# Phase two's full-array products issued as four tiles of 32 columns

## The chip, the cores and the metric

The kernel runs on one core of a Trainium2 chip. The metric is the device time of one execution in microseconds; lower is better. Times before are the median of three runs. The profile is one execution, recorded by the hardware profiler.

## What is computed

The input `x` has 8 sequences of 1024 tokens with 256 features. All is f32. Two blocks follow each other, each with a residual:

```python
x = x + attn_ref(layernorm(x))     # phase one: 16 heads, low-rank keys and values, causal
x = x + ffn_ref(layernorm(x))      # phase two: two layers, DEPTH = 2

def layer(x):                      # 8 heads of 64, windows of 128 tokens
    h = shift_token(x)             # second half of the features is taken from the token before
    q, k, v = split(h @ wqkv, 3)   # 256 -> 3 * 512
    q, k = rotary_xpos(l2norm(q) * qs, l2norm(k) * ks)
    o = local_attention(q, k, v)   # a window sees itself and the window before
    x = x + o @ wo                 # 512 -> 256
    h = layernorm(shift_token(x)) * g + b
    a, gate = split(h @ w1 + b1, 2)        # 256 -> 2 * 682
    return x + (a * gelu(gate)) @ w2 + b2  # 682 -> 256
```

Phase two's two layers over eight sequences are 16 passes. Each has 8 windows of 128 tokens for the attention (128 windows in all) and 2 chunks of 512 tokens for the MLP (32 chunks in all).

## The kernel before

Phase one (`mla`) takes about the first 967 us. Its dense products already go through a helper `times` (L199), which issues a product of 128 x 128 weights as four matmuls, one for each 32 columns of the weights, into the four 32-partition strips of the output. Its scores (L455) use 32 rows and 128 columns of the array, its values (L488) 128 rows and 32 columns.

Phase two (`local`) is the part that changes. A class `Pass` holds one layer of one sequence. Its methods work on a window `i`:

- `qk` (product at L886): q and k of the window, four products of 128 x 128 weights (the tokens, transposed, `left(i)`) with 512 moving columns of `wqkv`, into a PSUM pair buffer `pair`. ScalarE squares it (L891), VectorE multiplies by the rotary tables (L893, L896), GpSimd adds and scales (L900, L906).
- `transposes`: a turn on VectorE and a way through DRAM by SyncE's DMA queue (`turned`, `z`, `qkT`).
- `v` (L913): two such products, evacuated by ScalarE.
- `scores` (L958): 32 matmuls in tiles of 64 rows and 32 columns into two more turns of the pair buffers, which ScalarE reads with the exponential (L964).
- `values` (L999) and the sums of the softmax (L1007): 32 and 8 matmuls in tiles of 128 rows and 32 columns.
- `output` (L1032), once for two windows: 16 is the number of its recorded matmuls, 128 x 128 weights with 256 moving columns.

The MLP of a chunk is a generator, `mlp`, advanced in units between these: `up` (L1115), 128 x 128 weights with 512 moving columns, then Gelu (L1127) on ScalarE and the gated product (L1128) on VectorE; and the down projection `psy`, L1156 with 128 x 128 weights and 256 moving columns, and at its end the rest of the hidden features, L1162, which has 64 rows (one half of `rest_hid` for each of two sums).

The order on every compute engine is that of the program text (`tc.manual_schedule`). A step of the main loop works on several windows at once, each at another stage:

```python
each(step, "both", 4); each(step, "qk", 0); each(step, "transposes", 1); each(step, "v", 0)
next(units, None)             # a unit of the MLP
each(step, "values", 4)
each(step, "scores", 3)
made[j // NT].output(...)     # every second step
next(units, None)             # a unit of the MLP
```

So in each step TensorE goes from full-array products to `values`, its sums and `scores`, and back to full-array products. Two pair buffers (`pair0`, `pair1`) take turns for `qk` once and `scores` twice in a step; three banks (`mm`) serve v, the sums, output and the MLP. An f32 product appears in the profile as two matmuls and two weight loads.

Of the kernel before, what the change touches and what calls it, by code (L numbers as in the profile page):

```python
# [36 lines left out]
P = 128  # L37
# [21 lines left out]
INNER = HEADS * DH  # L59
# [23 lines left out]
def preln_mla_local_kernel(  # L83
# [27 lines left out]
    nc = tc.nc  # L111
# [12 lines left out]
    def rsqrt(out_, in_, n):  # L124

        nc.gpsimd.tensor_tensor(out_, in_, half[:, :n], ALU.pow)  # L126
# [527 lines left out]
    NF = HID // P  # L654
# [3 lines left out]
    def local(ctx: ExitStack, verdict):  # L658
# [4 lines left out]
        p1 = ctx.enter_context(tc.tile_pool(name="l1", bufs=1))  # L663
        p2 = ctx.enter_context(tc.tile_pool(name="l2", bufs=2))

        ppair = [ctx.enter_context(tc.tile_pool(name="pair0", bufs=1, space=PSUM))]
        psum = ctx.enter_context(tc.tile_pool(name="psum3", bufs=3, space=PSUM))
        ppair.append(ctx.enter_context(tc.tile_pool(name="pair1", bufs=1, space=PSUM)))
# [7 lines left out]
        rest_hid = p1.tile([P, CH // 2], F32, name="rest_hid")  # L676
# [12 lines left out]
        def load_attention(l):  # L689


            w = {}
            queue = nc.sync if l else nc.scalar
            w["qkv"] = wa.tile([P, 2, 3 * INNER], F32, tag="qkv", name=f"l_qkv{l}")
            nc.sync.dma_start(w["qkv"], wqkv[l].rearrange("(c p) e -> p c e", p=P))

            for name, src in (("cos", xpos_cos), ("sin", xpos_sin)):
                w[name] = wa.tile([P, NT, 2, DH], F32, tag=name, name=f"l_{name}{l}")
                queue.dma_start(w[name], src)
                f = wa.tile([P, 2, DH], F32, tag=f"f{name}", name=f"l_f{name}{l}")  # L700
                for i, sc_ in enumerate((q_scale, k_scale)):
                    if name == "cos":
                        queue.dma_start(f[:, i, :], sc_[l].partition_broadcast(P))
                    else:
                        queue.dma_start(f[:, i, :H], sc_[l, H:].partition_broadcast(P))
                        queue.dma_start(f[:, i, H:], sc_[l, :H].partition_broadcast(P))
                w[f"f{name}"] = f
            return w
# [156 lines left out]
        class Pass:  # L865
# [14 lines left out]
            def qk(self, i):  # L880
                key, w = self.key(i), self.w
                A, S = w["cos"], w["sin"]
                qk = next(turns).rearrange("p (n j) (m d) -> p n (j m) d", n=2, d=DH)
                for n in range(2):
                    for c in range(2):
                        nc.tensor.matmul(  # L886
                            qk[:, n].rearrange("p h d -> p (h d)"), self.left(i)[c],
                            w["qkv"][:, c, n * INNER : (n + 1) * INNER], start=(c == 0), stop=(c == 1),
                        )
                sq = p1.tile([P, 2, HEADS, DH], F32, tag="sq", name=f"sq{key}")  # L890
                nc.scalar.activation(sq, qk, AF.Square)  # L891
                t1 = p1.tile([P, 2, HEADS, DH], F32, tag="t1", name=f"t1{key}", bufs=2)
                nc.vector.tensor_tensor(t1, qk, A[:, i].unsqueeze(2).to_broadcast([P, 2, HEADS, DH]), ALU.mult)  # L893
                t2 = p1.tile([P, 2, HEADS, DH], F32, tag="t2", name=f"t2{key}")
                for lo, hi in ((0, H), (H, 0)):
                    nc.vector.tensor_tensor(  # L896
                        t2[:, :, :, lo : lo + H], qk[:, :, :, hi : hi + H],
                        S[:, i, :, lo : lo + H].unsqueeze(2).to_broadcast([P, 2, HEADS, H]), ALU.mult,
                    )
                nc.gpsimd.tensor_tensor(t1, t1, t2, ALU.add)  # L900
                ss = small.tile([P, 2, HEADS], F32, tag="ss", name=f"ss{key}")
                nc.vector.tensor_reduce(ss, sq, AX.X, ALU.add)
                nc.vector.tensor_scalar(ss, ss, 1e-24, None, ALU.max)
                rn = small.tile([P, 2, HEADS], F32, tag="rn", name=f"rn{key}")
                rsqrt(rn.rearrange("p i h -> p (i h)"), ss.rearrange("p i h -> p (i h)"), 2 * HEADS)
                nc.gpsimd.tensor_tensor(t1, t1, rn.unsqueeze(3).to_broadcast([P, 2, HEADS, DH]), ALU.mult)  # L906
                self.rot[i] = t1

            def v(self, i):
                key = self.key(i)  # L910
                pv = psum.tile([P, INNER], F32, tag="mm", name=f"pv{key}")
                for c in range(2):
                    nc.tensor.matmul(  # L913
                        pv, self.left(i)[c], self.w["qkv"][:, c, 2 * INNER :], start=(c == 0), stop=(c == 1)
                    )
                self.vs[i] = p1.tile([P, INNER], F32, tag="v", name=f"v{key}", bufs=6)
                evac(self.vs[i], pv)

# [105 lines left out]
            def output(self, n):  # L1024

                oT = self.oTs.pop(n)
                x_, y, key = self.x_, self.y, f"{self.b}_{self.l}"
                two = slice(2 * n, 2 * n + 2)
                ps = psum.tile([P, 2, D], F32, tag="mm", name=f"psw{key}_{n}")
                for i in range(2):  # L1030
                    for c in range(4):
                        nc.tensor.matmul(  # L1032
                            ps[:, i, :], oT[:, c, i * P : (i + 1) * P], self.w["o"][:, c, :],
                            start=(c == 0), stop=(c == 3),
                        )
                nc.vector.tensor_tensor(x_[:, two], ps, x_[:, two], ALU.add)  # L1036

                rows = slice(2 * n * P, (2 * n + 2) * P)
                nc.sync.dma_start(y[rows, :P].rearrange("(t p) d -> p t d", p=P), x_[:, two, :P])
                rows = slice(2 * n * P + 1, (2 * n + 2) * P + 1)  # L1040
                nc.sync.dma_start(y[rows, P:].rearrange("(t p) d -> p t d", p=P), x_[:, two, P:])
                m, o = divmod(2 * n + 2, ST)
                if o == 0:
                    self.hs[m - 1] = p2.tile([P, ST, D], F32, tag="h", name=f"h{key}_{m - 1}")
                    rows = slice((m - 1) * CH, m * CH)
                    nc.sync.dma_start(self.hs[m - 1], y[rows].rearrange("(t p) d -> p t d", p=P))
# [49 lines left out]
        def mlp():  # L1096


            w = load_mlp(0)
# [7 lines left out]
            for k, (q, n) in enumerate(chunks):  # L1107
                l, b, x_ = made[q].l, made[q].b, made[q].x_
                key = made[q].key(n)
                d = ds.pop(k)  # L1110

                def up(i):
                    ps = psum.tile([P, CH], F32, tag="mm", name=f"ag{key}_{i}")
                    for c in range(2):
                        nc.tensor.matmul(  # L1115
                            ps.rearrange("p (s a t) -> p s a t", a=4, t=32), w["1"][:, c, i, :],
                            d[:, c],
                            start=(c == 0), stop=(c == 1),
                        )
                    return ps  # L1120

                hid = p1.tile([P, NF, CH], F32, tag="hid", name=f"hid{key}")
                for i in range(NF):
                    gate = up(2 * i + 1)
                    a = up(2 * i)
# [14 lines left out]
                for g in range(2):  # L1140
                    cols = slice(CH // 2 * g, CH // 2 * (g + 1))
# [10 lines left out]
                for g, ps in enumerate(sums):  # L1152
                    for t in range(2):
                        cols = slice((2 * g + t) * P, (2 * g + t + 1) * P)
                        for i in range(NF):
                            nc.tensor.matmul(  # L1156
                                ps[:, t, :], hid[:, i, cols], w["2"][:, i, :], start=(t == i == 0), stop=False
                            )
                for t in range(2):
                    for g, ps in enumerate(sums):  # L1160
                        rows = slice(64 * g, 64 * g + 64)
                        nc.tensor.matmul(  # L1162
                            ps[:, t, :], rest_hid[rows, t * P : (t + 1) * P], w["2"][rows, NF, :], start=False,
                            stop=(t == 1),
                        )
                for g, ps in enumerate(sums):
                    part = slice(ST * n + 2 * g, ST * n + 2 * g + 2)
# [3 lines left out]
                    else:  # L1171
                        rows = slice(n * CH + 2 * g * P, n * CH + (2 * g + 2) * P)
# [4 lines left out]
                if k + 1 < len(chunks) and made[chunks[k + 1][0]].l > l:  # L1177
                    w = load_mlp(l + 1)
# [17 lines left out]
        w = load_attention(0)  # L1196
# [3 lines left out]
        ready = {0: first}  # L1200
        w["o"] = load_o(0)
        units = mlp()
        next(units)

# [7 lines left out]
        with tc.manual_schedule(engines={E.PE, E.DVE, E.Activation, E.Pool}):  # L1212
            for step in range(windows + LAG):
                n, i = divmod(step, NT)
                if step < windows and i == 0:
                    l, b = passes[n]
                    if n and b == 0:
                        o = w["o"]
                        w = load_attention(l)
# [556 lines left out]
    with ExitStack() as two:  # L1776
        local(two, verdict)
# [7 lines left out]
    with tc.tile_pool(name="psum_v", bufs=1, space=PSUM) as psum:  # L1785
        ps = psum.tile([1, 1], F32, name="psbad")
# [80 lines left out]
```

## Time and profile before

| | |
|---|---|
| median of three runs | 3293.98 us (3292.47 to 3296.29) |
| the profiled execution: time | 3292.07 us |
| its span, first to last instruction | 3290.3 us |
| mean granted TensorE clock | 0.994 |
| instructions | 79693 |
| recorded matmuls, and weight loads | 33762 each |
| phase two (967 us to the end) | 23458 matmuls, as many loads |

The full-array products of phase two, each group with its matmuls, its busy time and the mean length of one:

| line | product | matmuls | moving columns | busy us | mean ns |
|---|---|---|---|---|---|
| L1115 | MLP up | 1408 | 512 | 640.8 | 597 |
| L886 | q, k | 1024 | 512 | 466.7 | 599 |
| L1156 | MLP down | 1280 | 256 | 281.5 | 379 |
| L913 | v | 512 | 512 | 240.6 | 592 |
| L1032 | attention output | 1024 | 256 | 240.2 | 388 |
| L1162 | MLP down, rest (64 rows) | 256 | 256 | 36.3 | 402 |

PE is TensorE's matmuls, PEld its weight loads, which overlap with them. DVE is VectorE, ACT ScalarE, POOL GpSimd, SP SyncE. A matmul's length is longer than its share of the engine, since the next starts before it ends; so the distance from one start to the next is what tells its cost. In shapes like `128*32 128x512`, the first pair is the rows and columns of the array that are used, the second the moving operand.

### The profile page before, as it was taken

The page shows a single profiled execution, that of the slowest core. Times are in us where ns is not written, and L with a number is a line of the kernel's source. Part 1 is how long each engine was busy: PE and PEld are TensorE (multiplying, and loading weights), DVE is VectorE, ACT ScalarE, POOL GpSimd, SP SyncE. Part 2 cuts the span into 40 slices and gives each one's busy share as a digit, 9 for nine tenths or more (in the row PEclk, how much of TensorE's full clock was granted, in tenths as well). Part 3 has the DMA queues.
Part 4 walks back from the last instruction along what each step waited for, and adds up shares of the span by engine and source line. Part 5 has one row for each costly group of instructions (what it writes and reads, how often), then busy time and mean ns, then how long its engine had stood idle before and what let it go on. Part 6 is the DMA issues. An engine that isn't in the chain of part 4 may idle for free.

```text
span 3290.3 us, 79693 instructions
## 1 busy us (share of the span) xinstructions
PE 3196.2 (97%) x33762; PEld 1763.2 (54%) x33762; DVE 2668.6 (81%) x3934; ACT 1712.4 (52%) x2055; POOL 1342.9 (41%) x1064
## 2 busy tenths in 40 slices
PE   7999999999987999999999999999999999999998
PEld 2434343443334566656666656566666656665665
DVE  4999989998987887887878877787877778787773
ACT  6888888888742344444343444343443444444441
POOL 1000000000017755555555555565555555555540
PEclk9999999999998999999999999999999999999999
DMA  4133222313324344444445445454544535454431
GB/s 128 44 94 84 59 75 75 91 46 84 105 89 114 101 128 119 132 118 119 121 117 135 112 128 145 126 129 137 148 123 122 142 110 134 133 139 123 112 102 58
DMA packets 389771, 362.10 MB, mean 110 GB/s; under 512 B 158703, under 2 KB 337310, under 8 KB 389278
## 3 DMA queue, kind: packets, MB, share of 16 engines
q1 hardware_dynamic: 387422, 354.51, 39.8%
q8 instruction: 268, 4.39, 0.6%
q10 hardware_dynamic: 1984, 2.41, 0.2%
q14 instruction: 97, 0.79, 0.1%
HBM read 165.96 MB, written 140.51 MB: 93 GB/s over the span
## 4 chain that ended last, share of the span: by engine, by line
PE 84%; DVE 6%; ACT 4%; DMA 2%; issue 2%; SPq 1%; POOL 0%; ACTq 0%; DVEq 0%
PE ag L1115 17%; PE pair L886 13%; PE psy L1156 8%; PE psw L1032 7%; PE o L999 6%; PE acc L488 6%; PE pv L913 6%; PE sc L455 5%; PE pair L958 4%; DVE pt L477 3%; PE s L1007 2%; PE psx L201 2%; PE psq L201 1%; PE psR L201 1%; ACT pt L463 1%
## 5 line engine op out<-in xcount | busy, mean ns | idle before, releaser
L477 DVE TENSOR_TENSOR pt<-pt,er 128x1024 f32<-128x1024 f32 x576 | 671.7, 1221 | 35.8 <-ACT pt L463 35.7
L1115 PE MATMUL ag<-d,l 128*128 128x512 f32 x1408 | 640.8, 597 | 1.4 <-DVE xs L1036 0.8
L900 POOL TENSOR_TENSOR t<-t,t 128x1024 f32<-128x1024 f32 x128 | 302.0, 2360 | 791.5 <-DVE t L896 791.5
L463 ACT ACTIVATE pt<-sc 128x1024 f32<-128x1024 f32 x576 | 561.2, 1032 | 115.6 <-PE sc L455 105.9
L964 ACT ACT_TABLE_LOAD x120 | 154.0, 1283 | 701.2 <-PE pair L958 697.1
L886 PE MATMUL pair<-l_qkv,xT 128*128 128x512 f32 x1024 | 466.7, 599 | 5.7 <-DMA xT<-zx 2.8
L1115 PEld LDWEIGHTS ag<-d,l 128*128 128x128 f32 x1408 | 262.0, 190 | 311.0 <-issue 276.9
L126 POOL TENSOR_TENSOR rn<-ss,half 128x16 f32<-128x16 f32 x128 | 373.4, 2917 | 13.8
L488 PE MATMUL acc<-pt,v 128*32 128x512 f32 (+3 forms) x3072 | 345.6, 496 | 11.2 <-DVE pt L477 10.0
L886 PEld LDWEIGHTS pair<-l_qkv,xT 128*128 128x128 f32 x1024 | 193.1, 191 | 247.5 <-issue 208.8
L891 ACT ACTIVATE sq<-pair 128x1024 f32<-128x1024 f32 x128 | 131.1, 1024 | 330.7 <-issue 256.5
L893 DVE TENSOR_TENSOR t<-pair,l_cos 128x1024 f32<-128x1024 f32 x128 | 156.3, 1221 | 155.6 <-ACT sq L891 155.0
L1156 PE MATMUL psy<-l,hid 128*128 128x256 f32 x1280 | 281.5, 379 | 0.0
L1128 DVE SCALAR_TENSOR_TENSOR hid<-ag,l_b,ge 128x512 f32<-128x512 f32 x160 | 115.9, 724 | 195.4 <-ACT ge L1127 170.4
L1156 PEld LDWEIGHTS psy<-l,hid 128*128 128x128 f32 x1280 | 243.2, 190 | 46.7 <-issue 15.1
L964 ACT ACTIVATE pt<-pair 128x1024 f32<-128x1024 f32 (+1 forms) x256 | 235.0, 968 | 57.1 <-PE pair L958 55.8
L906 POOL TENSOR_TENSOR t<-t,rn 128x1024 f32<-128x1024 f32 x128 | 249.1, 1946 | 10.0
L455 PE MATMUL sc<-q,k 32*128 32x512 f32 (+3 forms) x3072 | 245.1, 380 | 4.4 <-ACT pt L463 3.3
L999 PEld LDWEIGHTS o<-pt,v 128*32 128x32 f32 x7680 | 201.6, 110 | 88.0 <-issue 82.0
L913 PE MATMUL pv<-l_qkv,xT 128*128 128x512 f32 x512 | 240.6, 592 | 0.0
L1032 PE MATMUL psw<-l_o,oT 128*128 128x256 f32 x1024 | 240.2, 388 | 0.0
L999 PE MATMUL o<-pt,v 128*32 128x128 f32 x7680 | 237.0, 274 | 2.6 <-POOL pt L966 2.4
(324 smaller groups left out, 4604.0 us busy)
## 6 DMA issues: line engine op xcount, KB each, us to landing
z<-turned SPq DMA_DIRECT2D x512, 128.0 KB, 2.4
qkT<-z SPq DMA_DIRECT2D x128, 512.0 KB, 3.6
y<-xs SPq DMA_DIRECT2D x128, 128.0 KB, 3.4
h<-y SPq DMA_DIRECT2D x32, 512.0 KB, 4.3
zx<-turneds SPq DMA_DIRECT2D x120, 128.0 KB, 2.4
xT<-zx SPq DMA_DIRECT2D x240, 64.0 KB, 2.6
zh<-turnedh SPq DMA_DIRECT2D x120, 128.0 KB, 2.3
d<-zh SPq DMA_DIRECT2D x30, 512.0 KB, 3.2
```

The source lines that it names most:

```text
L126: nc.gpsimd.tensor_tensor(out_, in_, half[:, :n], ALU.pow)
L455: nc.tensor.matmul(two[n // 2][:, n % 2, lo : lo + w], k[rows], q[rows, h], start=(h == 1), stop=(h == 0),)
L463: nc.scalar.activation(pt, sc, AF.Exp, scale=SCALE)
L477: nc.vector.tensor_tensor(t, t, er.to_broadcast([P, 1024 // w, w]), ALU.mult)
L488: nc.tensor.matmul(self.acc[g][32 * n : 32 * n + 32, q0 - c * 512 :], self.v[:, kb, h * VW : h * VW + 32], pts[n // 2][:, n % 2, lo : lo + w],
L886: nc.tensor.matmul(qk[:, n].rearrange("p h d -> p (h d)"), self.left(i)[c], w["qkv"][:, c, n * INNER : (n + 1) * INNER], start=(c == 0), s ...
L913: nc.tensor.matmul(pv, self.left(i)[c], self.w["qkv"][:, c, 2 * INNER :], start=(c == 0), stop=(c == 1))
L964: nc.scalar.activation(pt[:, :, : n * P], flat[:, :, : n * P], AF.Exp, scale=-1.0)
L999: nc.tensor.matmul(o[32 * j : 32 * j + 32, g, a, :], vs[m][:, h * DH + a * 32 : h * DH + a * 32 + 32], pts[m][g][:, place(j), off : off + ...
L1032: nc.tensor.matmul(ps[:, i, :], oT[:, c, i * P : (i + 1) * P], self.w["o"][:, c, :], start=(c == 0), stop=(c == 3),)
L1115: nc.tensor.matmul(ps.rearrange("p (s a t) -> p s a t", a=4, t=32), w["1"][:, c, i, :], d[:, c], start=(c == 0), stop=(c == 1),)
L1156: nc.tensor.matmul(ps[:, t, :], hid[:, i, cols], w["2"][:, i, :], start=(t == i == 0), stop=False)
```

## The change

`local` gets its own `times`, the same as that of phase one, and every product that used all 128 columns is issued through it. The weights' 128 columns are taken 32 at a time, and the output's partitions likewise; the moving operand, the accumulation and the order of the products stay. The tiles have 128 rows and 32 columns, and for L1162 64 rows and 32 columns.

```diff
+        QUARTER = [slice(32 * n, 32 * n + 32) for n in range(4)]
+
+        def times(out, w, rhs, start, stop):
+            for four in QUARTER:
+                nc.tensor.matmul(out[four], w[:, four], rhs, start=start, stop=stop)
+
...
                 for n in range(2):
                     for c in range(2):
-                        nc.tensor.matmul(
+                        times(
                             qk[:, n].rearrange("p h d -> p (h d)"), self.left(i)[c],
-                            w["qkv"][:, c, n * INNER : (n + 1) * INNER], start=(c == 0), stop=(c == 1),
+                            w["qkv"][:, c, n * INNER : (n + 1) * INNER], c == 0, c == 1,
                         )
...
                 for c in range(2):
-                    nc.tensor.matmul(
-                        pv, self.left(i)[c], self.w["qkv"][:, c, 2 * INNER :], start=(c == 0), stop=(c == 1)
-                    )
+                    times(pv, self.left(i)[c], self.w["qkv"][:, c, 2 * INNER :], c == 0, c == 1)
...
                 for i in range(2):
                     for c in range(4):
-                        nc.tensor.matmul(
-                            ps[:, i, :], oT[:, c, i * P : (i + 1) * P], self.w["o"][:, c, :],
-                            start=(c == 0), stop=(c == 3),
-                        )
+                        times(ps[:, i, :], oT[:, c, i * P : (i + 1) * P], self.w["o"][:, c, :], c == 0, c == 3)
...
                     for c in range(2):
-                        nc.tensor.matmul(
-                            ps.rearrange("p (s a t) -> p s a t", a=4, t=32), w["1"][:, c, i, :],
-                            d[:, c],
-                            start=(c == 0), stop=(c == 1),
+                        times(
+                            ps.rearrange("p (s a t) -> p s a t", a=4, t=32), w["1"][:, c, i, :], d[:, c],
+                            c == 0, c == 1,
                         )
...
                         for i in range(NF):
-                            nc.tensor.matmul(
-                                ps[:, t, :], hid[:, i, cols], w["2"][:, i, :], start=(t == i == 0), stop=False
-                            )
+                            times(ps[:, t, :], hid[:, i, cols], w["2"][:, i, :], t == i == 0, False)
                 for t in range(2):
                     for g, ps in enumerate(sums):
                         rows = slice(64 * g, 64 * g + 64)
-                        nc.tensor.matmul(
-                            ps[:, t, :], rest_hid[rows, t * P : (t + 1) * P], w["2"][rows, NF, :], start=False,
-                            stop=(t == 1),
+                        times(
+                            ps[:, t, :], rest_hid[rows, t * P : (t + 1) * P], w["2"][rows, NF, :], False, t == 1
                         )
```

## The prediction

> **What bounds the kernel now.** I read four views: the page's busy table, the stretches, the chain of waits, and the timeline of TensorE. Phase one ends and phase two begins at about 967 us; the second line below is the table of stretches cut there, its columns being span, then busy time and instructions of PE, PEld, DVE, ACT, POOL.
>
> ```profile
> PE 3196.2 (97%) x33762; PEld 1763.2 (54%) x33762; DVE 2668.6 (81%) x3934; ACT 1712.4 (52%) x2055; POOL 1342.9 (41%) x1064
> ...
> PE 84%; DVE 6%; ACT 4%; DMA 2%; issue 2%; SPq 1%; POOL 0%; ACTq 0%; DVEq 0%
> ```
> ```profile
> 967.00:3290.00 2323.00, 2283.49 (x23458) 1396.28 (x23458) 1814.14 (x2864) 932.91 (x1013) 1263.61 (x932) 0.99 0.44 122
> 1100.00:3200.00 2100.00, 2095.53 (x21726) 1282.43 (x21725) 1671.81 (x2636) 880.12 (x949) 1160.00 (x858) 1.00 0.46 126
> ```
>
> From 1100 to 3200 us PE is busy for 2095.5 of 2100 us, and the next engine, DVE, for 1672 (80%). The chain is 84% PE. So PE sets the time of phase two, at full clock (1.00), and a nanosecond taken off PE is one off the span, unless a wait turns up in its place. But busy is not the same as full speed. The timeline (start us, length us, what) shows where PE is slower than its own steady pace. One window's stretch in phase two:
>
> ```profile
> 2015.29 1.13 PE L1162 MATMUL psy<-l,rest_hid 64*128 64x256 f32 x8
> 2016.35 1.95 PE L999 MATMUL o<-pt,v 128*32 128x128 f32 x64
> 2018.12 0.62 PE L1007 MATMUL s<-both,ones_l 128*32 128x128 f32 x16
> 2018.67 1.32 PE L958 MATMUL pair<-qkT 64*32 64x160 f32 x64
> 2019.92 3.72 PE L1032 MATMUL psw<-l_o,oT 128*128 128x256 f32 x16
> 2023.48 3.60 PE L886 MATMUL pair<-l_qkv,xT 128*128 128x512 f32 x8
> 2026.91 1.88 PE L913 MATMUL pv<-l_qkv,xT 128*128 128x512 f32 x4
> 2028.63 3.60 PE L1115 MATMUL ag<-d,l 128*128 128x512 f32 x8
> 2032.15 1.96 PE L999 MATMUL o<-pt,v 128*32 128x128 f32 x64
> ```
>
> Read start to start, since lengths overlap. An f32 product is two recorded matmuls. L886 takes 3.43 us for 8: 429 ns each, its steady pace at 512 columns; at 256 the trace's starts are 216 apart. L1115 takes 3.52 us for the same 8, 93 more: after it L999 uses another shape of the array (128*128 to 128*32). L1032 takes 3.56 us where 16 x 216 is 3.46: its first matmul holds PE 104 ns longer, having been entered from another shape, so its weight load was not hidden. L999 after such an entry takes 1.77 us for 16 rounds of four at 109, which is 24 more: its loads have 32 columns. L1162 has both ends, 1.06 us for four rounds of 215.
>
> And phase one, where products are already issued as four tiles:
>
> ```profile
> 604.14 1.05 PE L201 MATMUL psx<-wout,oT 128*32 128x256 f32 x16
> 605.00 1.04 PE L436 MATMUL reach<-sq,ones_m 128*32 128x512 f32 x8
> 605.97 0.75 PE L455 MATMUL sc<-q,k 32*128 32x256 f32 x16
> ```
>
> 16 tiles of 256 columns take 0.86 us, with no change of shape after them: 215 ns for each four. 8 tiles of 512 take 0.97 with a change after them: 2 x 429 + 0.11 (93 for the change, 20 for the stagger of the last four). Taken one by one, starts in phase one are 7 ns apart within a four, and fours are 429 or 216 apart: the pace of the full array.
>
> **What the skill says.** The Trainium skill, "TensorEngine Tiling (Array Packing)", Key Properties: "Changing tiling mode (not just tile) drains the TensorE". The trace agrees and prices it: 93 ns on every such change. "TensorE: Matmul & The Clock Gate", LDWEIGHTS: a load costs its column count over 1.2, so 107 ns at 128 columns and 27 at 32; the exposed loads above are 104 and 24. The same page, Part 3 (packing), has tiles in different column strips running together, about 4 ns apart; the trace has them together, 7 apart.
>
> **The change part by part.** A "round" is one pass through PE: one full matmul now, four tiles afterwards.
>
> 1. *Steady pace.* Full matmuls by the groups: 1408 + 1024 + 1280 + 1024 + 512 = 5248 become 20992, and L1162's 256 become 1024: 16512 more matmuls and as many loads. Rounds stay 5248, at 429 or 216 ns either way: cost 0. What hides four times the instructions is their concurrency. Phase one doesn't show the moving pattern of L1115 (runs of 32 elements), but L958 reads such runs in eight tiles together at 136 ns a round for 160 columns, no slower in proportion. Bounds: a round 1 ns shorter or 2 ns longer, -5 to +10 us; I take 0.
>
> 2. *Into L999.* Each of 128 windows has L999, L1007, L958. Into L999 PE comes 98 times from a full product, which will then have the same shape: drain 93 and exposed load 24 go, 98 x 117 = 11.5 us. In 30 windows it comes from L1162, which keeps a shape of its own (64*32 hereafter), so nothing goes.
>
> 3. *Out of L958.* 64*32 to full becomes 64*32 to 128*32: the drain stays, the exposed load falls from 104 to 24. The trace counts 130 such entries: 130 x 80 = 10.4 us. No row has 64*32 to 128*32; nearest are 64*128 to 128*32 (93 + 24) and 128*32 to 64*32 (93 + 24), so I take 93 + 24.
>
> 4. *L1162.* Still entered over a drain, but with 32-column loads: 32 x 80 = 2.6 us. Its 64-row halves must still run together in eight tiles as L958's do; if one half trailed by a round, it would cost 32 x 215 ns = 6.9 us. Bounds -2.6 to +4.3; I take the gain.
>
> 5. *Waits after L958.* In 28 windows the q, k product waits for the pair buffer that the exponential still reads:
>
> ```profile
> PE pair L958 <- DMA qkT<-z: 15.1, 4, 9.4
> ```
> ```profile
> PEld pair L886 <- ACT pt L964: 31.7, 55, 1.2
> ```
>
> (Waited for: us in total, times, longest.) The first is the largest of PE's waits in phase two, for item 6; the second, from 1100 to 3200 us, is that of L886's weight loads; behind it the whole PE queue stands, v and the next unit of the MLP. The 80 ns of item 3 come after L958, so here PE only arrives earlier and waits longer: -28 x 80 ns = 2.2 us lost. But each restart exposes its load too (104 more in 28 rounds of L886), now 24: 2.2 us won back. Net 0. Item 2 comes before L958 and moves the exponential as well, so it isn't absorbed.
>
> 6. *Start of phase two.* The four waits for qkT, 15.1 us, are mostly a chain of DMAs before the first windows. Some five windows' worth of 0.2 us vanishes there: +1 us.
>
> DMAs, their order on SP, and the work of DVE, ACT and POOL are unchanged. The only added traffic is instructions: see the slower rival.
>
> Sum: -11.5 - 10.4 - 2.6 + 0 + 1 = -23.5 us. The profiled execution took 3292.07 us (span 3290.3 and 1.8 around it), so 3268.6; it lies 1.9 below the median of the runs, 3293.98, and from that I get **3270.5 us** (-0.7%). About 0.2%, 6.6 us, is what a measurement of this kernel can tell from no change.
>
> **Rivals.**
>
> *A: waits take it back.* PE's cover is thin after L958: ACT's table load (1283 ns) and two exponentials (971 each) follow it, and only some windows have slack. If all of item 3 and half of item 2 ended in waits, 23.5 falls to 7.4: 3286.6. For it: the 55 waits on that buffer. Against it: they sum to only 31.7 us, most windows have an output or more of the MLP between, and DVE is idle a fifth of the time.
>
> *B: slower; instructions arrive too late.* Phase two has 23458 matmuls and as many loads in 2323 us, 20 instructions a us; with 16512 more of each it is 34. The instruction queue (q8) moved 4.39 MB in 268 packets for 67524 PE instructions, so 16 KB and some 250 instructions a packet, at 0.6% of 16 engines: 1.2 us each. Needed hereafter is one in 7 us. That speaks against it, as does the burst of 144 matmuls and 144 loads in 3.6 us (L999 to L958) at 80 a us. For it: no stretch of 100 us has over 25 a us now. It decides below 34 a us; at 33.5, phase two's 79940 would take 2386 us, 63 longer than now: 3357. A milder form is a round that is longer by tile overhead: the saving is gone at 23.5 us over 5248 rounds, 4.5 ns each; at 7 ns it is +37 - 23.5, or 3307.
>
> *C: the tiles don't run together.* Each four would take four rounds, thousands of us in all. The same helper in phase one (0.86 us for 16 tiles) excludes it.
>
> **How the numbers follow.** Forecast 0.75, A 0.15, B 0.1, C 0. The forecast's own range is 3262 (a round 1 ns shorter and some waits shorter) to 3281 (rounds 2 ns longer). A extends it to 3287; B is left out. Range 3262 to 3287. Faster by over 0.2% means below 3287.4: the forecast and most of A, 0.86. Within 0.2%: 0.05. Slower: 0.09.
>
> **What would show it.** PE has 50274 matmuls. Before L999, eight matmuls of L1115 become 32 in 3.43 us instead of 3.52; L1032 after L958 takes 3.48 instead of 3.56; L1162 has 32 in 0.98 instead of 1.06 (1.2 or more if its halves trail). L886's loads waiting for ACT stay near 32 us; at 45 or more, A is at work. Rounds of 436 or 223, or PE idle for issue, would mean B. The forecast is wrong if fours in phase two are over 4 ns longer than full matmuls, or if L958 to a 128*32 tile costs more than 93 + 24.

## The result, and the profile after

The changed kernel takes 3275.4 us, median of six runs (3272.52 to 3276.37), against 3293.22 for the kernel before in six: ratio 0.9942, 95% interval 0.9932 to 0.9953, a gain of 17.8 us. The forecast was 3270.5 (23.5 us of gain) with a range of 3262 to 3287. The profiled execution has a span of 3273.5 us, 16.8 less than before.

The busy table and the chain of waits of the changed kernel:

```profile
PE 3177.2 (97%) x50274; PEld 1456.0 (44%) x50274; DVE 2671.1 (82%) x3934; ACT 1712.5 (52%) x2055; POOL 1341.6 (41%) x1064
...
PE 84%; DVE 6%; ACT 4%; DMA 3%; issue 2%; SPq 1%; POOL 0%; ACTq 0%; DVEq 0%; POOLq 0%
```

The 16512 added matmuls are there (33762 to 50274), with their loads. PE lost 19 us of busy time and its weight loads (PEld) 307; VectorE, ScalarE and GpSimd changed by under 3. The chain is still 84% PE: no other engine took over. Phase two as one stretch (start and end, span, then busy time of PE, PEld, DVE, ACT, POOL, with their instructions, the granted clock, and the DMA share and rate):

```profile
967.00:3273.00 2306.00, 2264.21 (x39970) 1088.57 (x39970) 1816.21 (x2863) 933.21 (x1013) 1262.30 (x932) 0.99 0.45 124
```

PE handles 39970 matmuls and as many loads in 2306 us, 35 instructions a us. The timeline of PE (start us, length us, what) in the place that answers to the one shown of before:

```profile
2005.63 1.09 PE L670 MATMUL psy<-l,rest_hid 64*32 64x256 f32 x32
2006.65 1.95 PE L1003 MATMUL o<-pt,v 128*32 128x128 f32 x64
2008.42 0.62 PE L1011 MATMUL s<-both,ones_l 128*32 128x128 f32 x16
2008.97 1.45 PE L962 MATMUL pair<-qkT 64*32 64x160 f32 x64
2010.35 3.66 PE L670 MATMUL psw<-l_o,oT 128*32 128x256 f32 x64
2013.83 3.62 PE L670 MATMUL pair<-l_qkv,xT 128*32 128x512 f32 x32
2017.26 1.90 PE L670 MATMUL pv<-l_qkv,xT 128*32 128x512 f32 x16
2018.98 3.62 PE L670 MATMUL ag<-d,l 128*32 128x512 f32 x32
2022.41 1.93 PE L1003 MATMUL o<-pt,v 128*32 128x128 f32 x64
2024.16 0.62 PE L1011 MATMUL s<-both,ones_l 128*32 128x128 f32 x16
```

All the products now have the line of the helper, L670, so the tiles' names tell them apart. Start to start: q, k take 3.43 us as before, now in 32 matmuls; v 1.72 in 16. The MLP's up product ahead of the values (`ag`) takes 3.43 instead of 3.52: its drain is gone. The values after it take 1.75 instead of 1.77: their first loads are hidden. The output (`psw`) after the scores takes 3.48 instead of 3.56: its first load has 32 columns. The rest (`rest_hid`) takes 1.02 instead of 1.06, where 0.98 was forecast.

### The profile page after: what moved, and what is told of

Its sections match the earlier page's. It is cut to its first block, busy times and chain, and to the rows that moved or that the text cites. A ratio compares the mean times of both kernels' runs of the same rounds, so it can differ in the third digit from the quotient of the medians.

```text
span 3273.5 us, 112729 instructions
## 1 busy us (share of the span) xinstructions
PE 3177.2 (97%) x50274; PEld 1456.0 (44%) x50274; DVE 2671.1 (82%) x3934; ACT 1712.5 (52%) x2055; POOL 1341.6 (41%) x1064
## 4 chain that ended last, share of the span: by engine, by line
PE 84%; DVE 6%; ACT 4%; DMA 3%; issue 2%; SPq 1%; POOL 0%; ACTq 0%; DVEq 0%; POOLq 0%
PE ag L670 17%; PE pair L670 13%; PE psy L670 9%; PE psw L670 7%; PE acc L488 7%; PE pv L670 6%; PE o L1003 6%; PE sc L455 5%; PE pair L962 4%; DVE pt L477 3%; PE s L1011 2%; PE psx L201 2%; PE psq L201 1%; PE psR L201 1%; ACT pt L463 1%
## 5 line engine op out<-in xcount | busy, mean ns | idle before, releaser
L670 PE MATMUL ag<-d,l 128*32 128x512 f32 x5632 | 639.8, 593 | 0.7 <-ACT d L1085 0.4
L670 PE MATMUL pair<-l_qkv,xT 128*32 128x512 f32 x4096 | 468.3, 597 | 6.6 <-ACT pt L968 3.2
L670 PEld LDWEIGHTS ag<-d,l 128*32 128x32 f32 x5632 | 179.0, 110 | 384.0 <-issue 362.0
L670 PE MATMUL psy<-l,hid 128*32 128x256 f32 x5120 | 282.1, 379 | 0.0
L670 PEld LDWEIGHTS pair<-l_qkv,xT 128*32 128x32 f32 x4096 | 132.6, 111 | 307.8 <-issue 252.5
L1003 PEld LDWEIGHTS o<-pt,v 128*32 128x32 f32 x7680 | 212.8, 110 | 72.7 <-issue 68.9
L670 PE MATMUL pv<-l_qkv,xT 128*32 128x512 f32 x2048 | 244.1, 592 | 0.0
L670 PE MATMUL psw<-l_o,oT 128*32 128x256 f32 x4096 | 240.2, 386 | 0.1
L420 POOL TENSOR_SCALAR_AFFINE_SELECT er<-er 128x128 f32<-128x128 f32 x64 | 39.1, 610 | 480.7 <-ACT er L418 480.7
```

What stands on the lines that cost most here:

```text
L670: nc.tensor.matmul(out[four], w[:, four], rhs, start=start, stop=stop)
L1003: nc.tensor.matmul(o[32 * j : 32 * j + 32, g, a, :], vs[m][:, h * DH + a * 32 : h * DH + a * 32 + 32], pts[m][g][:, place(j), off : off + ...
```

## The experiments

Every kernel shared its chip with runs of the kernel before, and gains are against those. Where a stage's length is given, it is the distance from its first matmul to that of the next stage, taken stage by stage in both traces. The runs of the kernel before in these comparisons have medians of 3293.9 to 3295.1 us, so compare gains or ratios and not the bare times.

**v as a full product again.** From the changed kernel:

```diff
-                    times(pv, self.left(i)[c], self.w["qkv"][:, c, 2 * INNER :], c == 0, c == 1)
+                    nc.tensor.matmul(
+                        pv, self.left(i)[c], self.w["qkv"][:, c, 2 * INNER :], start=(c == 0), stop=(c == 1)
+                    )
```

> The changed kernel with one product put back: v is one full-array product again, q, k before it and the MLP after it stay tiled, so each of 128 windows gets two more changes of shape. Theory (the gain is changes of shape, and loads exposed by them): into v 93 ns of drain and 104 of exposed 128-column load, out of it 93 + 24, 314 ns in all, x 128 = 40 us: about 3315 us against 3275.4, slower even than before the change (3293.2). Rival (tiling makes each product cheaper at its steady pace): v is 220 us of about 2050 us of tiled products, so it loses about a ninth of the 17.8 us: 3277 us.

Measured: 3319.01 us, ratio 1.0076 (1.006 to 1.0093), 23.9 slower than the kernel before and 41.7 behind the changed kernel's gain. The rival, a share of one ninth, is excluded. Its timeline:

```profile
2236.38 3.64 PE L670 MATMUL pair<-l_qkv,xT 128*32 128x512 f32 x32 [0.40 <-ACT pt L970]
2239.95 1.98 PE L919 MATMUL pv<-l_qkv,xT 128*128 128x512 f32 x4
2241.87 8.84 PE L670 MATMUL psy<-l,hid 128*32 128x256 f32 x160
2250.64 1.09 PE L670 MATMUL psy<-l,rest_hid 64*32 64x256 f32 x32
```

v, four matmuls, takes 1.92 us between changes of shape instead of 1.72 with none: 104 of exposed load and 93 of drain. In all windows' stages, q, k lengthen by 113 ns (93 of drain and 20 of the last four's stagger, the time from the start of the first of the four to that of the last), v by 198, and the stage after by 24. That is 335 x 128 = 43 us; the stages of phase two together are 41.9 longer than in the changed kernel's trace. A single product of the other shape, in an otherwise tiled phase, costs more than twice what the whole change gained.

**The change of shape moved, not removed.** From the changed kernel, in the main loop and the helper:

```diff
-            for four in QUARTER:
+            for four in QUARTER if tiled[0] else [slice(0, P)]:
...
+                tiled[0] = True
                 if not late:
                     each(step, "v", 0)
...
                 each(step, "values", 4)
+                tiled[0] = False
                 each(step, "scores", 3)
```

> Tiles only from v to the values of a step: v, and the unit of the MLP between v and the values (up or down projection with its rest), are four tiles; q, k, the output and the unit of the MLP after the scores are full products. So PE still changes shape three times a window, before v instead of before the values. Theory (changes of shape): no gain, 3293 us, within 2 us of the kernel before; the trace has no drain before the values, and 93 + 24 ns before v. Rival (steady pace of tiled products): about half the time of the products is tiled, so about half the gain, 3284 us. Second rival (it is the values' entry itself that counts, whatever comes before): 98 x 117 ns = 11.5 us of gain, 3282 us.

Measured: 3301.39 us, ratio 1.0022 (1.0013 to 1.0031): slower than before by 6.3. About half of phase two's product time is tiled here, and nothing of the gain is left, so neither rival holds: it isn't a cheaper pace of tiles, nor the values' entry by itself.

```profile
2244.04 3.60 PE L672 MATMUL pair<-l_qkv,xT 128*128 128x512 f32 x8
2247.57 1.92 PE L672 MATMUL pv<-l_qkv,xT 128*32 128x512 f32 x16
2249.31 3.62 PE L672 MATMUL ag<-d,l 128*32 128x512 f32 x32
2252.74 1.93 PE L1005 MATMUL o<-pt,v 128*32 128x128 f32 x64
```

The drain is now behind q, k (3.53 us for 3.43) and the exposed load in v (1.74 for 1.72), while `ag` ahead of the values is down to 3.43. The expectation of no change was wrong by a count. The drain is added in all 128 windows but taken off in 98, since in 30 the rest of the down projection stands between and keeps its own shape. 30 x 117 ns = 3.5 us explains half of the loss. The stages of phase two are 7.0 us longer than before; the other 3.5 are waits and stagger, of which 1.6 lie at the change of layer.

**The rest of the down projection back to 64 x 128.**

```diff
-                        times(
-                            ps[:, t, :], rest_hid[rows, t * P : (t + 1) * P], w["2"][rows, NF, :], False, t == 1
-                        )
+                        nc.tensor.matmul(
+                            ps[:, t, :], rest_hid[rows, t * P : (t + 1) * P], w["2"][rows, NF, :], start=False,
+                            stop=(t == 1),
+                        )
```

> The changed kernel with the rest of the down projection (64 rows) put back to 64 x 128 tiles. As the prediction had it, each of 32 chunks loses 80 ns by exposed loads of 128 columns: +2.6 us. As the two traces read: eight tiles start 7 ns apart and end so, which gave 40 of the 80 back, so the stage from the rest to the values is 40 ns longer here than in the changed kernel, 1.3 us in all: 3276.7 us, which a time can't tell from 3275.4, but the trace can.

Measured: 3279.25 us, ratio 0.9955 (0.9938 to 0.9971), 15.9 faster than the kernel before. As foreseen, the time can't tell it from the changed kernel. The trace can (the rest, and the values that follow it):

```profile
2296.68 1.14 PE L1160 MATMUL psy<-l,rest_hid 64*128 64x256 f32 x8
2297.74 1.95 PE L1003 MATMUL o<-pt,v 128*32 128x128 f32 x64
```

1.06 us, against 1.02 with eight tiles, in each of the 30 stages that lead to the values: 1.2 us in all. All stages of phase two together are 4.4 us longer here, most of it in the first windows; two traces of the changed kernel itself differ by about 3.

**Scores ahead of the values where the rest precedes them.** The finding suggests a better order. Where the rest (64 x 32) comes just before the values (128 x 32), and the scores (64 x 32) just after, turning those two round saves two changes of shape. Every compute engine follows the order of the program text, so the turn also moves the exponential of the scores and what follows the values on the other engines (`rests` is filled in `mlp` where the rest is issued, and emptied before each unit ahead of the values):

```diff
+                rests.append(k)
...
-                each(step, "values", 4)
-                each(step, "scores", 3)
+                two = [("values", 4), ("scores", 3)]
+                if rests:
+                    two.reverse()
+                    rests.clear()
+                for name, back in two:
+                    each(step, name, back)
```

> The changed kernel with one order turned round, only in the 30 steps where the down projection's rest (64 x 32 tiles) comes ahead of the values: there the scores (64 x 32 as well) are issued before the values. PE then changes shape into the rest, out of the scores, and no more: two changes instead of four in such a step. Theory (a change of shape costs 93 ns of drain, 24 of exposed load, and 20 to 46 of stagger of the tiles before it): two changes fewer, 0.25 to 0.28 us x 30 = 7.5 to 8.5 us less than the changed kernel, near 3267.5. Rival (what is left of the time is waits for data, so a shape change saved ends in a wait for the pair buffer or for qkT): no gain, 3275.

> The same turn of the order in every step: scores before values. Outside the 30 steps the number of changes of shape stays two. Theory (changes of shape): the gain of the kernel that turns the order in 30 steps only, and not more; less than that by what the scores wait for the pair buffer, which VectorE reads for q, k until about 3.8 us after q, k end, 1.4 us before the scores would start. So 3267 to 3285. Rival (the gain is the earlier exponential, which frees the pair buffer sooner for the next q, k): clearly more gain here than in the 30 steps, 3260 or less.

Measured: with the turn in 30 steps, 3273.13 us, ratio 0.9936 (0.9923 to 0.995), a gain of 21.1 us; with the turn in every step 3281.22, ratio 0.9963 (0.995 to 0.9976), a gain of 13.0. The changed kernel, on the same chip, had 3276.59, ratio 0.9946 (0.9931 to 0.9961), a gain of 17.6. So the first is faster than the changed kernel by 3.5 us, but their intervals overlap. The timeline of the first:

```profile
2009.20 1.09 PE L670 MATMUL psy<-l,rest_hid 64*32 64x256 f32 x32
2010.09 1.32 PE L962 MATMUL pair<-qkT 64*32 64x160 f32 x64
2011.34 1.96 PE L1003 MATMUL o<-pt,v 128*32 128x128 f32 x64
2013.11 0.62 PE L1011 MATMUL s<-both,ones_l 128*32 128x128 f32 x16
2013.55 3.64 PE L670 MATMUL psw<-l_o,oT 128*32 128x256 f32 x64
```

The rest takes 0.89 us and the sums 0.44, since no drain follows either, and the output that comes next loses its exposed load: 0.27 us less in each such step, as the theory had it. In the stretch from the 32nd to the 62nd output this is 4.1 us for its 15 such steps. But the stretch is only 2.2 shorter than in the changed kernel: four of its stages of the sums, one of the values and one of the output are 0.2 to 0.9 longer, so nearly half of what is saved ends in waits. (Two traces of the changed kernel differ by 0.3 in this stretch, two of the kernel before by less than 0.1.)

The turn in every step is slower as a whole than the changed kernel, by the medians, but its trace keeps the rival, the earlier exponential, alive. In that same stretch it is 8.0 us shorter than the changed kernel, and the weight loads of q, k there hardly wait for the exponential any more (0.3 us from 2130 to 3170 us, where the changed kernel's second trace has 18.6). It loses where the pipeline is disturbed. From 967 to 1180 us, in the first windows, PE waits 16.6 us for qkT, against 1.9 in that second trace; some other waits are shorter there, and all together are 36.3 us against 27.9. At the change of layer it waits once more:

```profile
2050.28 2.39 PE L962 MATMUL pair<-qkT 64*32 64x160 f32 x64 [5.65 <-DMA qkT<-z]
```

So the turn gains more than changes of shape where the steps run evenly, and loses where they don't. The next pair makes the turn in the even steps alone, tiled and untiled.

**Scores first, but for the first windows and the change of layer.** In the changed kernel, and in the same way in the kernel before:

```diff
-                each(step, "values", 4)
-                each(step, "scores", 3)
+                two = [("values", 4), ("scores", 3)]
+                if step >= 12 and not 63 <= step <= 66:
+                    two.reverse()
+                for name, back in two:
+                    each(step, name, back)
```

> The changed kernel with the scores ahead of the values from step 12 on, but for steps 63 to 66. Turned in every step, the order was 8.0 us shorter than the changed kernel in the stretch of 30 outputs in the second layer, but lost more than that to waits for qkT and the pair buffer in the first eight windows and in the one at the change of layer; those are left as they were here. Theory (two changes of shape fewer in 30 steps, and an earlier exponential, which frees the pair buffer for the next q, k): twice that stretch's gain, 14 to 16 us less than the changed kernel, a ratio near 0.990 against the kernel before, 3261. Rival (the waits move on to the windows after, as they did with the turn in 30 steps, where half of the gain went): 5 to 8 us less, a ratio near 0.9925.

> The kernel before, its products untiled, with the same turn of the order in the same steps. The number of changes of shape stays what it was (three in a step, four in one with the rest of the down projection, since its 64 x 128 tiles differ from the scores' 64 x 32). Theory (of the gain by the turned order in tiled form, 8 us are changes of shape and the rest is the earlier exponential): only the latter shows, 6 to 8 us less than the kernel before, a ratio near 0.998. Rival (all of the turn's gain is changes of shape): same as before, 0.9995 to 1.0005. Second rival (all of it is the earlier exponential): 14 to 16 us, near 0.9955.

Measured: tiled 3266.32 us, ratio 0.9926 (0.9912 to 0.9939), 27.6 us faster than the kernel before by the medians; untiled 3288.39, ratio 0.9983 (0.9976 to 0.9989), 5.5 faster. The first has the lowest median of all versions. Its runs spread from 3261.8 to 3273.8, and the intervals of its ratio and the changed kernel's (0.9932 to 0.9953) just overlap. Its gain over the changed kernel, 10 us by the medians, lies between the theory's 14 to 16 and the rival's 5 to 8. Untiled, 5.5 us with an interval of some 4 to 8 leaves out both rivals (nothing, and 14 to 16).

In the stretch from the 32nd to the 62nd output the parts are clear: 1059.4 us before, 1054.5 with the turn alone, 1050.0 with the tiles alone, 1041.9 with both (and 1041.9 with the tiles and the turn in every step). The turn gives 4.9 us untiled and 8.1 tiled. The 3.2 more are put down to changes of shape, which only the tiles make to go; by the count above these were worth 4.1.

The waits of q, k's weight loads for the exponential, from 1100 to 3200 us (us in total, times, longest), of the changed kernel, of the tiled one with the turn, and of the untiled one with the turn:

```profile
PEld pair L670 <- ACT pt L968: 37.3, 55, 1.3
```
```profile
PEld pair L670 <- ACT pt L968: 1.6, 3, 1.0
```
```profile
PEld pair L886 <- ACT pt L964: 1.1, 2, 0.9
```

In the kernel before they were 31.7 us. So the earlier exponential takes this wait away with the tiles or without them.

**Second traces of both kernels.** No edit.

> The changed kernel itself once more, for a second trace. If the faster PE systematically pays a wait where the layer changes (2.9 us longer there in the first pair of traces, 2018 to 2055 us) and in the first eight windows, this trace has it too against either trace of the kernel before. If those waits are the luck of single executions, the sums of these two stretches differ between the two traces of one kernel by as much as between the kernels, 1 to 3 us.

> The kernel before itself once more, for a second trace: the waits of the first eight windows and of the change of layer, against its first trace. If the waits are luck, these sums differ by 1 to 3 us between the two traces; if they are a property of the faster PE, they agree within 0.5 us.

The kernel before had 3298.07 in its single run. Its trace agrees with the first within 0.02 us in the two undisturbed stretches, 1110 to 2018 and 2055 to 3210 us, and differs by 2.5 in the first eight windows and by 1.7 at the change of layer, so waits in these two places vary from one execution to the next. Gains of the changed kernel by stretch, for the first pair of traces and the second:

| stretch of the kernel before, us | windows | first pair | second pair |
|---|---|---|---|
| 967 to 1110 | 8 | -1.0 | -1.7 |
| 1110 to 2018 | 51 | -8.4 | -8.0 |
| 2018 to 2055, change of layer | 3 | +2.9 | +2.8 |
| 2055 to 3210 | 65 | -9.7 | -10.2 |
| 3210 to the end | 1 | -1.1 | -1.2 |

On the same stages of the change of layer, two traces of one kernel differ by 1.7 (before) and 1.6 (changed). Each of the four ways to pair the traces shows a loss there, of 1.3 to 4.5 us, where 0.5 was to be gained; so there is a loss, but its size is uncertain. It reads so in the first trace of before, and in that of the changed kernel:

```profile
2044.56 0.68 PE L1007 MATMUL s<-both,ones_l 128*32 128x128 f32 x16
2046.96 1.32 PE L958 MATMUL pair<-qkT 64*32 64x160 f32 x64 [1.72 <-DMA qkT<-z]
2048.21 3.72 PE L1032 MATMUL psw<-l_o,oT 128*128 128x256 f32 x16
2052.06 3.99 PE L1115 MATMUL ag<-d,l 128*128 128x512 f32 x8
```
```profile
2035.48 0.94 PE L1011 MATMUL s<-both,ones_l 128*32 128x128 f32 x16 [0.70 <-DVE both L987]
2039.26 1.32 PE L962 MATMUL pair<-qkT 64*32 64x160 f32 x64 [2.85 <-DMA qkT<-z]
2040.51 5.35 PE L670 MATMUL psw<-l_o,oT 128*32 128x256 f32 x64
2045.68 3.62 PE L670 MATMUL ag<-d,l 128*32 128x512 f32 x32
```

The sums now wait for VectorE (0.70 us), the scores for qkT 2.85 instead of 1.72, and the output (`psw`) takes 5.17 us instead of 3.85.

**No reload of the attention weights.** In both kernels the second layer's load of its attention weights is left out, with the scaling of its rotary tables and the later place of q, k and v in its first window; that layer then works with the first layer's weights:

```diff
-                    if n and b == 0:
-                        o = w["o"]
-                        w = load_attention(l)
-                        w["o"] = o
...
-                late = step < windows and n and i == 0 and b == 0
+                late = False
```

> The kernel before without the attention weights of the second layer: the first layer's wqkv and its scaled rotary tables serve both (this part of the computation is changed), so neither their three loads nor the scaling nor the late place of q, k, v in the first window of that layer. Compared with its partner below, with four tiles. Between the fourth output and the end of the change of layer the kernel before took 76 us for the two outputs around the change; without the reload about 71 (four windows of 17.7). So about 3289 us.

> The changed kernel with the same part left out. Theory (some 4 us of the expected gain end in waits around the reload of the layer's weights): without the reload the gain against the kernel before without it is about 21 us, so 3268 us if that one is at 3289, and the waits for qkT and for both in the windows around the change are gone in both. Rival (the waits there belong to the pipeline itself or to the DMAs of x, at this place in every run): the gain stays near 17.8, 3271.

Measured: 3291.15 us untiled, ratio 0.9989 (0.9982 to 0.9996), and 3271.95 tiled, ratio 0.9933 (0.9916 to 0.9949). The gain between the two is 19.2 us, between the theory's 21 and the rival's 17.8, and the times are too coarse to part it from the latter. The traces, one of each, say more: the stages of phase two differ by 19.4 us instead of 17.3 and 18.3, and those of 2018 to 2055 us by -0.5 instead of +2.9 and +2.8. In the tiled kernel no stage there waits:

```profile
2039.64 1.93 PE L1003 MATMUL o<-pt,v 128*32 128x128 f32 x64
2041.39 0.62 PE L1011 MATMUL s<-both,ones_l 128*32 128x128 f32 x16
2041.94 1.32 PE L962 MATMUL pair<-qkT 64*32 64x160 f32 x64
2043.18 3.66 PE L670 MATMUL psw<-l_o,oT 128*32 128x256 f32 x64
```

So the loss at that place hangs on the reload or on the order that goes with it. Which of the two it is, and why the tiled kernel waits longer there, was not taken apart.

## Why the prediction was right, and where its sizes were off

The direction and the mechanism held: PE sets the time, and the gain is drains and exposed loads at changes of shape, not a faster product. The kernel that put changes of shape back and the one that moved them lost it.

1. *Steady pace, taken as 0.* Right. Stages with no change at either end are equal within 1 ns: 29 of v before the down projection and 86 before the up projection sum to 0.0 us.
2. *Into L999, 11.5 us.* Right: 98 stages before the values are 93 ns shorter, and where nothing else waits the values are 24 shorter, 92 times.
3. *Out of L958, 10.4 us.* Right: 80 ns less at 117 to 122 entries, 9.4 to 9.7 us. 64*32 to 128*32, of which no row was known, costs what the neighbours cost.
4. *L1162, 2.6 us.* Mis-sized: it measured 0.6. The step left out the stagger, though it was in the text for phase one. The stage became 40 ns shorter instead of 80, and the down projection before it 20 ns longer: net 20 ns x 32. The starts fit this: eight tiles 7 ns apart start, and so end, some 40 ns later than two, and four some 20 later than one. With the rest back at 64 x 128 the stage is 40 ns longer again.
5. *Waits after L958, net 0.* Right. In 28 stages of q, k that begin after such a wait, the first load's exposed part is 80 ns shorter, and in as many stages of the MLP ahead of them the 80 are waited away. The weight loads of q, k waited 37.3 us for the exponential, after 31.7, less than the 45 set as the mark of rival A. The wait is real, though: the turned order took it away.
6. *The first windows, +1.* Not borne out as such; eight windows gained 1.0 and 1.7 us in the two pairs, where 1.4 was to be had; two traces of one kernel differ there by 1.7 to 2.5. The waits came elsewhere, and were not in the sum: some 3.3 us at the change of layer (+2.8 instead of -0.5), and in the first pair, scattered over the rest, more that changes from trace to trace.

The sum closes for the first pair: items 2 and 3 gave 21.3 us, item 4 gave 0.6, and stages that fit none of these amounts lost 4.6. That is the 17.3 us by which phase two's stages are shorter. Of the 23.5 forecast, 6.2 are missing: 3.6 are waits beyond the 1 allowed for them, 2.0 are item 4, and 0.6 are items 2 and 3. So the prices were right but for item 4, and the forecast was too high mainly because it took nearly every saving to reach the end.

Rival A, waits that take the gain back, was at work only in part: 4.6 us of some 22, and mostly not in the wait for the pair buffer that it named. Rival B, instructions that come too late, fell clearly: 35 a us and 397 packets on the instruction queue, 6.50 MB (399 follow from 268 by the instruction counts), with the pace unchanged. Rival C too: rounds of four run at 429 and 216 ns.

## What to carry to other kernels

On a TensorE-bound path, look for the places where consecutive matmuls use different shapes of the array, and price each one from start-to-start distances: here 93 ns of drain, plus the load of the first weights, 104 or 24 ns by their columns, plus the stagger of the tiles before it. Count changes per loop, not products: tiling a product pays only if it leaves fewer changes, and one product left in the other shape can cost more than all the others gained. Then ask which wait stands next where the loop is disturbed: here the saving, the same in every step, was lost at the change of layer, and the order that suited the even steps was the wrong one in the first windows.

## What the runs showed of the hardware that was not expected

Two things, of which the second had been an open question. The stagger within a group of tiles, 6.5 to 7 ns from one to the next, costs nothing from round to round, but appears in full at a change of shape: 20 ns after four tiles, about 40 more after eight than after two. And PE took 35 instructions a us through phase two, after 20, with no round longer for it.
